# First layer: the first half's share of the second half's taps computed from PSUM, with a new order and new shares for the scan

## The chip, the cores and the metric

The kernel runs on one core of a Trainium2 chip. A core has five engines that work side by side, each through its own instructions in program order: TensorE (PE, matrix products and transposes, which land in PSUM), VectorE (DVE), ScalarE (ACT), GpSimd (POOL, which here works on SBUF alone) and SyncE (SP, which here issues the DMAs). In the profile, PEld is TensorE's loading of the stationary operand, which overlaps its products. The metric is the device time of one execution in microseconds (us).

## The reference, cut to what matters

Two layers run one after the other on `x`, float32 of shape (4, 512, 32, 32): four batches, 512 channels, 1024 positions. The change lies in the first one, a selective scan (Mamba) block with 1024 inner channels and 16 states.

```python
xz = xn @ W_in                                   # xn: normalized x, (B, L, 512)
xm, z = (xz[..., :d_inner], xz[..., d_inner:])
xc = conv_general_dilated(xm.transpose(0, 2, 1), conv_w[:, None, :], (1,), [(D_CONV - 1, 0)],
                          ..., feature_group_count=d_inner)   # 4 causal taps, channel by channel
xs = silu((xc + conv_b[None, :, None]).transpose(0, 2, 1))
proj = xs @ W_x
dt = softplus(proj[..., :dt_rank] @ W_dt + b_dt)
Bm = proj[..., dt_rank:dt_rank + D_STATE]
Cm = proj[..., dt_rank + D_STATE:]
A = -exp(A_log)
def step(h, inp):
    dt_t, B_t, C_t, x_t = inp
    dA = exp(dt_t[..., None] * A)
    h = dA * h + (dt_t * x_t)[..., None] * B_t[:, None, :]
    y = einsum('bds,bs->bd', h, C_t)
    return (h, y)
y = ys.transpose(1, 0, 2) + xs * D_param         # ys: the scan's y over all L positions
y = y * silu(z)
out = y @ W_out
```

Its output is added to `x`. The second layer (a position attention block with two 3x3 convolutions, which the kernel computes in a transformed form) follows.

## The kernel before, in words

**Tiling.** The 1024 inner channels are eight chunks `d` of 128 partitions. A pair of chunks is `e` (0 to 3), `j` tells the two of a pair apart, and the 1024 positions are two halves `h` of 512. The scan of a batch runs in eight stages, `n = 2e + h`, and each stage in 16 units, one for each state `s`; that makes 32 stages and 512 units. Products y are collected over the 16 states in two PSUM tiles by TensorE, with transposes that accumulate (line 985), and at a stage's end ScalarE copies them out (line 1008).

**A unit** needs exp(dt·A) (ScalarE, line 899), dt·x·B, the scan (DVE, two instructions at line 952), and the product with C. There are choices:
- dt·x·B is made by ScalarE in a transposed layout (four scalings, line 912) and turned by TensorE into PSUM (tile `u`, line 938), or by one POOL product over both chunks (line 927), for which B comes in by a broadcast DMA (tile `bbc`).
- The product with C, which a broadcast DMA brings (tile `cbc`), is one POOL instruction over both chunks (line 975) or two of DVE (line 968). For the first half, the scan's last column is kept in `carry_sb`, by POOL (line 974) or DVE (line 957).

How many of a stage's 16 units go by ScalarE is in the table `ACT_B` (a row for each batch, a column for each stage). How many of the others have their product with C on DVE is in `DVE_C`. The function `shares` spreads them over the states.

**The causal taps.** The first batch is started by halves: `conv1_half(d, h, prio)` projects a half of a chunk into PSUM (line 445, tile `pxm`), makes the tap without shift on ScalarE from PSUM into `u`, adds the three shifted taps on DVE (line 747) and applies SiLU (line 760). The first three positions of the second half need the last three columns of the first half. ScalarE keeps them in an SBUF tile `tails` (line 741), and when the second half comes, DVE adds their parts with three small instructions (line 752). The first halves of all chunks run first, and the second halves later, in between the first scan stage. The other batches are projected in one go by `conv1`, in three column ranges, with SiLU (line 719) for groups of chunks whose size is `PRM["xp"]`.

**Order.** All first-layer work is handed to a `Plan`. Each `step` names its engine, a cost in us, what it reads and writes, a priority (smaller is sooner), and the buffers that it holds. `Plan.issue` then runs a list schedule with these costs when the program is built, and emits the instructions in the order in which the schedule starts them. On the chip each engine keeps that order, whatever the true durations are. Priorities come from `PRM`: `kt`, `ke` and `ka` for how far the transposes, the exponentials and the additions to y lie ahead of their unit, `dl` for the deltas, `m0`, `c0`, `cg` and `p0` for the next batch's normalization and projections, `g0` and `gg` for the gates, `o0` and `og` for the output projection, `pc` for the 18 weight transforms of the second layer that are made in the first, `h0` and `hg` for the first batch's second halves, `l3` to `l6` and `fi` for the end. `TURN` and `URGENT` weigh a change of ScalarE's function table against the priority of what waits. The costs, such as `MM` (a matmul of 512 columns), `TR` (a transpose of 128), `ROWS` (two scalings), `EXP` and `SCAN`, stand in the code as numbers.

The second layer (lines from 1280 on) is written in plain order and runs after the first.

Of the kernel before, what the change touches and what calls it, by code (L numbers as in the profile page):

```python
# [15 lines left out]
P = 128  # L16
# [12 lines left out]


PRM = dict(
    xp=(2, 2, 1),
    d1=8.23,
    pg=(0.7, 0.35, 0.47, 0.46),
    kt=(1.13, 4.81, 2.25, 3),
    ke=(2.14, 5.78, 2.26, 3.85),
    ka=(-5.03, -1.69, -3.51, -2.93),
    dl=(11.85, 12.29, 12.5, 13.83),
    nl=(0.29, 0.79, 0.92),
    m0=(52.82, 51.61, 54.43),  # L40
    c0=(70.47, 60.11, 59.82),
    cg=(4.54, 5.65, 6.27),
    p0=(115.27, 106.44, 113.51),
    g0=(-0.87, -46.47, -49.33, -53.09),
    gg=(7.9, 8.99, 9.46, 7.52),
    o0=(15.94, 15.36, 9.69),
    og=(5.82, 6.15, 7.12),
    pc=(-120.93, -9.27, -95.57, -42.69, -26.91, -49.06, -36.73, 11.76, 16.43, 53.49, 94.05, 153.95, 217.99, 261.76, 328.41, 365.53, 443.31, 500.69),
    h0=-5.26,
    hg=2.44,  # L50
    p1=2.25,
    d2=-9.17,
    fl=0,
    fi=-3.13,
    l3=74.31,
    l5=104.57,
    l6=109.5,
)


ACT_B = (
# [4 lines left out]
)  # L66
DVE_C = (
# [4 lines left out]
)  # L72


# [22 lines left out]
class Plan:  # L97
# [5 lines left out]
    HOP = {"PE": 0.16, "DVE": 0.045, "ACT": 0.06, "POOL": 0.08, "SP": 0.05}  # L103
    BEGIN = {"PE": 5.0, "DVE": 1.5, "ACT": 9.0, "POOL": 7.0, "SP": 1.5}
    FREE, LOAD, SLACK, AHEAD = 0.06, 1.3, 0.11, 15.44
    TURN, URGENT = 2.11, 2.89

    def __init__(self, slots, in_order, exp_set):
        self.slots, self.steps, self.exp_set = dict(slots), [], exp_set
# [106 lines left out]
def mamba_then_pab_kernel(  # L216
# [105 lines left out]
    with ExitStack() as l0:  # L322
# [49 lines left out]


        carry_sb = wp.tile([P, 2, NS], F32, tag="carry", name="carry_sb")
        tails = wp.tile([P, NDC, 3], F32, tag="tails", name="tails")
        work = cpool.tile([P, NCC * (HH + 2) * (WW + 2)], F32, tag="image", name="work")
        proj_sb = wp.tile([P, L], F32, tag="proj", name="proj")
        nc.gpsimd.memset(proj_sb, 0.0)
# [19 lines left out]
            ("xt", "u", "h", "cbc", "bb", "dbx", "sc"), exp_set,  # L398
        )
        step = plan.step  # L400
        MM, TR = 0.858, 0.109
        ROWS, EXP, SCAN = 0.8, 0.613, 1.12

        def buf(ring, shape, name, free=False):
            if ring is None:
# [23 lines left out]

        xts, ready, xs, xh, dts = {}, {}, {}, {}, {}  # L430
        pieces = buf(None, None, "")
        tail = [buf(None, None, "") for d in range(NDC)]
        cells, at = {}, 0
        for ring, rows in (("tg", 9), ("tm", 6), ("tp", 6), ("tn", 6), ("to", 4), ("to", 4)):
            cells.setdefault(ring, []).append(work[:, at * QC : (at + rows) * QC])
# [16 lines left out]
        def norms(b, prio, lag=0.0):  # L452
# [167 lines left out]
            def scaled(c, h):  # L620
                hs = halves[h]
                step(
                    "DVE", 0.61,
                    lambda: nc.vector.scalar_tensor_tensor(
                        t()[:, c, hs], t()[:, c, hs], spl["nb"][:, c : c + 1], pvars[h](),
                        ALU.add, ALU.mult,
                    ),
                    [pvars[h], by_half[h]], [by_chunk[c][h]], prio, holds=[t],
                )
# [54 lines left out]
        def conv1(b, d, prio):  # L684

            w = load_win(b, d, prio)
            new_xs(b, d)
            u, xsh = xs[b, d], xh[b, d]
            cw = tap_weights(d)
            for at, end in ((0, 341), (341, 682), (682, L)):  # L690
                before = min(at, 3)
                n = end - at
                name = f"pxm_{b}_{d}_{at}"

                p = project(b, d, w, name, slice(at - before, end), prio, holds=[u])

                def tap(at=at, end=end, before=before, p=p):
                    nc.scalar.activation(
                        u()[:, at:end], p()[:, before : before + end - at], AF.Copy, scale=cw[0]
                    )  # L700

                step("ACT", 0.09 + n / 1000, tap, [p], xsh, prio, holds=[u])

                def taps(at=at, end=end, before=before, p=p):
                    for k in range(1, 4):
                        first = max(at, k)
                        nc.vector.scalar_tensor_tensor(  # L707
                            u()[:, first:end],
                            p()[:, first - k - at + before : end - k - at + before],
                            cw[k], u()[:, first:end], ALU.mult, ALU.add,  # L710
                        )

                step("DVE", 0.25 + n * 0.0037, taps, [p], xsh, prio, holds=[u])
        def silus(b, ds, prio):

            def several():
# [9 lines left out]
        def conv1_half(d, h, prio):  # L726

            if h == 0:
                new_xs(0, d)
            w, u, hs = load_win(0, d, prio), xs[0, d], halves[h]  # L730
            cw, me = tap_weights(d), [xh[0, d][h]]
            name = f"pxm_0_{d}_{h}"
            p = project(0, d, w, name, hs, prio, None if h else buf("u", [P, T], name, free=True), holds=[u])
            step(
                "ACT", 0.6,
                lambda: nc.scalar.activation(u()[:, hs], p(), AF.Copy, scale=cw[0]),
                [p], me, prio, holds=[u],
            )
            if h == 0:
                step(  # L740
                    "ACT", 0.2, lambda: nc.scalar.copy(tails[:, d], p()[:, T - 3 : T]),
                    [p], [tail[d]], prio,
                )

            def taps():
                for k in range(1, 4):
                    nc.vector.scalar_tensor_tensor(  # L747
                        u()[:, hs.start + k : hs.stop], p()[:, : T - k], cw[k],
                        u()[:, hs.start + k : hs.stop], ALU.mult, ALU.add,
                    )  # L750
                    if h:
                        nc.vector.scalar_tensor_tensor(
                            u()[:, T : T + k], tails[:, d, 3 - k :], cw[k],
                            u()[:, T : T + k], ALU.mult, ALU.add,
                        )

            step("DVE", 2.3 + 0.4 * h, taps, [p, *([tail[d]] if h else [])], me, prio, holds=[u])
            step(
                "ACT", 0.6,
                lambda: nc.scalar.activation(u()[:, hs], u()[:, hs], AF.Silu, bias=cb_sb[:, d : d + 1]),  # L760
                [], me, prio, "silu", holds=[u],
            )
# [118 lines left out]
        def unit(b, e, h, s, y):  # L881
# [50 lines left out]
            for j, u in enumerate(us):  # L932
                part = parts[j]
                if on_act:

                    def turn(j=j, u=u):
                        for k in range(NK):
                            nc.tensor.transpose(  # L938
                                u()[:, k * P : (k + 1) * P], sc()[:, k, j, :], ident
                            )  # L940

                    step(
                        "ACT", EXP, lambda j=j: decay(j, hc()[:, j]), [dt], [part], prio, "exp",
                        holds=[hc],
                    )
                    step("PE", 4 * TR, turn, [sc], [u], prio - PRM["kt"][b])
                else:
                    step("ACT", EXP, lambda j=j, u=u: decay(j, u()), [dt], [u], prio - PRM["ke"][b], "exp")

                def scan(j=j, u=u):  # L950
                    ht = u() if on_dve else hc()[:, j]
                    nc.vector.tensor_tensor_scan(  # L952
                        ht, *((hc()[:, j], u()) if on_act else (u(), hc()[:, j])),
                        carry_sb[:, j, s : s + 1] if h else 0.0, ALU.mult, ALU.add,
                    )
                    if h == 0 and on_dve:
                        nc.vector.tensor_copy(carry_sb[:, j, s : s + 1], ht[:, T - 1 : T])

                before, behind = ([carry[s][j]], []) if h else ([], [carry[s][j]] if on_dve else [])
                step(  # L960
                    "DVE", SCAN + (0.07 + 0.08 * (1 - h)) * on_dve, scan,
                    [part if on_act else hc, u, *before],
                    [u if on_dve else part, *behind], prio - 1, holds=[hc],
                )
                if on_dve:
                    step(
                        "DVE", 0.585,
                        lambda j=j, u=u: nc.vector.tensor_mul(hc()[:, j], u(), c_bc()[:, 0]),
                        [u, c_bc], [part], prio, holds=[hc],
                    )  # L970
            if not on_dve:
                def times_c():
# [2 lines left out]
                    nc.gpsimd.tensor_mul(hc(), hc(), c_bc().to_broadcast([P, 2, T]))  # L975

                step(
                    "POOL", 2.31 if h else 2.57, times_c,
                    [c_bc], [*parts, *([] if h else carry[s])], prio, holds=[hc],
                )  # L980
            for j in range(2):
# [237 lines left out]
        def transform(u, src, k, prio):  # L1219
# [16 lines left out]
            def scales():  # L1236
# [11 lines left out]
                [ends], [plus], prio, fill=True,  # L1248
            )
            step(  # L1250
                name, 1.76, lambda: eng.tensor_sub(minus(), plus(), mids()),
                [plus, mids], [minus], prio, fill=True,
            )
            step(
# [530 lines left out]
```

## Time and profile before

| | us |
|---|---|
| median of three runs | 2914.6 (2913.56 to 2916.33) |
| the profiled execution's own time | 2918.99 |
| its span, first to last instruction | 2917.2 |
| first layer, up to the first product of the second at 1892.8 | about 1893 |

The mean granted clock of TensorE is 0.983 of full speed. In the profile a group's row gives the line, engine, operation, tiles and shape, the count, the busy time and mean ns of one, and then the engine's idle time just before these instructions with what ended it. A row of waits has the engine and what it was to do, the work that released it, and the time in total, the times and the longest one. Tiles have the names of the program without numbers: `da` and `dbx` are a unit's SBUF tile (by ScalarE's way and by POOL's), `u` its PSUM tile.

### The profile page before, as it was taken

To read this page: it belongs to the slowest core of one execution; us is meant where nothing else is said; L and a number is where in the kernel's file an instruction comes from. 1 tells how busy PE (TensorE), PEld (TensorE's weight loads), DVE (VectorE), ACT (ScalarE), POOL (GpSimd) and SP (SyncE) were. 2 spreads that over 40 slices of the span, in tenths; PEclk is the share of its full clock that TensorE was granted. 3 is DMA by queue.
4 is the path that set the end of the run, shared out by engine and by line. 5 is a ranking of instruction groups with operands and counts; after the bars stand their busy time and mean duration, and the time that the engine had idled before them with its cause. 6 is when DMAs were issued, how large, how long until landed. Compare 5 with 4: busy or idle time off the path is not lost.

```text
span 2917.2 us, 36268 instructions
## 1 busy us (share of the span) xinstructions
PE 2728.5 (94%) x11744; PEld 1622.6 (56%) x11744; DVE 2315.5 (79%) x2762; ACT 1826.1 (63%) x3253; POOL 2001.9 (69%) x1217
## 2 busy tenths in 40 slices
PE   6798889999999999999999989799999999999998
PEld 3356566666666666666666766544444444444444
DVE  4579999998999989999899999867776755346254
ACT  4779899998989999989999999530300003030000
POOL 6889999889979999987999999733141341224222
PEclk9999899999999999999999999999999999999999
DMA  6665656568646578645576654667788896536487
GB/s 188 190 171 171 188 156 180 160 192 260 206 130 177 158 221 245 217 135 170 170 231 212 197 153 148 165 223 260 250 279 290 309 329 240 192 131 230 171 315 256
DMA packets 405829, 602.90 MB, mean 207 GB/s; under 512 B 47144, under 2 KB 246056, under 8 KB 381064
## 3 DMA queue, kind: packets, MB, share of 16 engines
q1 hardware_dynamic: 398024, 586.33, 63.3%
q10 hardware_dynamic: 7616, 14.26, 1.4%
q8 instruction: 94, 1.54, 0.2%
q14 instruction: 95, 0.78, 0.1%
HBM read 503.48 MB, written 96.99 MB: 206 GB/s over the span
## 4 chain that ended last, share of the span: by engine, by line
PE 33%; DVE 12%; ACT 4%; DMA 4%; POOL 3%; issue 2%; SPq 0%; DVEq 0%; POOLq 0%; ACTq 0%
PE m_o L1575 11%; PE m_b L1575 8%; PE pat L1627 4%; DVE da L952 3%; PE y L985 2%; PE po L445 2%; PE u L938 2%; DVE u L952 1%; POOL da L975 1%; ACT sc L912 1%; DVE xs L707 1%; PE psc L1427 1%; ACT da L899 1%; DMA u_o<-wo 1%; DMA uw_o<-u_o 1%
## 5 line engine op out<-in xcount | busy, mean ns | idle before, releaser
L975 POOL TENSOR_TENSOR da<-da,cbc 128x1024 f32<-128x1024 f32 x317 | 749.4, 2370 | 48.3 <-DVE da L952 26.6
L912 ACT ACTIVATE sc<-dtxt,bt_sb 128x256 f32<-128x256 f32 x1268 | 554.6, 497 | 35.4 <-PE u L938 34.4
L927 POOL TENSOR_TENSOR dbx<-dtx,bbc 128x1024 f32<-128x1024 f32 x195 | 461.1, 2375 | 31.7 <-PE y L985 21.6
L899 ACT ACTIVATE da<-dt,a_sb 128x512 f32<-128x512 f32 x634 | 436.5, 713 | 13.6 <-PE y L985 9.6
L938 PE MATMUL u<-ident,sc 128*128 128x128 f32 x2536 | 374.5, 280 | 50.7 <-DVE da L952 33.1
L938 PEld LDWEIGHTS u<-ident,sc 128*128 128x128 f32 x2536 | 294.8, 143 | 194.8 <-issue 51.3
L952 DVE TENSOR_TENSOR_SCAN da<-da,u 128x512 f32<-128x512 f32 x330 | 384.9, 1203 | 22.7 <-PE u L938 13.4
L952 DVE TENSOR_TENSOR_SCAN da<-da,carry_sb,u 128x512 f32<-128x512 f32 x304 | 372.9, 1261 | 16.5 <-PE u L938 9.5
L985 PE MATMUL y<-ident,da 128*128 128x128 f32 x2536 | 346.9, 277 | 26.1 <-POOL da L975 25.1
L1575 PE MATMUL m_o<-uw_o,v_o 128*128 128x512 f32 x768 | 335.4, 596 | 9.7 <-DMA uw_o<-u_o 9.7
L985 PEld LDWEIGHTS y<-ident,da 128*128 128x128 f32 x2536 | 294.3, 143 | 85.0 <-POOL da L975 42.1
L1575 PE MATMUL m_b<-uw_b,v_b 128*128 128x512 f32 x768 | 333.8, 593 | 5.7 <-DMA uw_b<-u_b 2.5
L899 ACT ACTIVATE u<-dt,a_sb 128x512 f32<-128x512 f32 x390 | 259.3, 682 | 18.8 <-DVE da L952 10.8
L445 PE MATMUL pxm<-xt,winc 128*128 128x345 f32 (+3 forms) x704 | 244.9, 490 | 13.0 <-DVE xs L707 3.8
L445 PE MATMUL pz<-xt,winc 128*128 128x512 f32 x512 | 243.1, 607 | 13.0 <-DVE xs L747 6.5
L1575 PEld LDWEIGHTS m_o<-uw_o,v_o 128*128 128x128 f32 x768 | 145.0, 191 | 191.6 <-issue 176.2
L1575 PEld LDWEIGHTS m_b<-uw_b,v_b 128*128 128x128 f32 x768 | 144.8, 190 | 191.2 <-issue 176.2
L1627 PE MATMUL pat<-y_b,st 128*128 128x512 f32 x512 | 223.3, 597 | 1.8 <-DVE rz L1636 1.8
L985 PE MATMUL y<-ident,dbx 128*128 128x128 f32 x1560 | 215.6, 277 | 10.0 <-POOL dbx L975 7.4
L985 PEld LDWEIGHTS y<-ident,dbx 128*128 128x128 f32 x1560 | 182.3, 143 | 39.4 <-issue 19.5
L1583 ACT ACTIVATE e_o<-m_o 128x512 f32<-128x512 f32 x24 | 14.3, 598 | 275.7 <-PE m_o L1575 261.3
L445 PE MATMUL po<-gt,wpr 128*128 128x512 f32 x384 | 182.5, 596 | 1.4 <-PE y L985 0.6
(225 smaller groups left out, 4241.6 us busy)
## 6 DMA issues: line engine op xcount, KB each, us to landing
cbc<-bcd SPq DMA_DIRECT2D x512, 256.0 KB, 3.7
uw_b<-u_b SPq DMA_DIRECT2D x96, 1024.0 KB, 4.8
uw_o<-u_o SPq DMA_DIRECT2D x96, 1024.0 KB, 4.7
bbc<-bcd SPq DMA_DIRECT2D x195, 256.0 KB, 4.3
u_b<-work SPq DMA_DIRECT2D x192, 128.0 KB, 3.1
winc<-in_w_in_dram SPq DMA_DIRECT2D x72, 256.0 KB, 3.9
szd<-sz SPq DMA_DIRECT2D x32, 512.0 KB, 4.5
szl<-szd SPq DMA_DIRECT2D x32, 512.0 KB, 4.9
```

The lines of the kernel that those rows point to most:

```text
L445: lambda k=k, lhs=lhs, rhs=rhs: nc.tensor.matmul(p()[:, at : at + cols], lhs(), rhs(), start=(k == 0), stop=(k == n - 1)),
L707: nc.vector.scalar_tensor_tensor(u()[:, first:end], p()[:, first - k - at + before : end - k - at + before], cw[k], u()[:, first:end], ALU ...
L899: nc.scalar.activation(t, dt()[:, j], AF.Exp, scale=a_sb[:, at : at + 1])
L912: nc.scalar.activation(sc()[:, k], dtxt()[:, k], AF.Copy, scale=bt[:, at, s : s + 1])
L927: lambda: nc.gpsimd.tensor_mul(hc(), dtx(), b_bc().to_broadcast([P, 2, T])),
L938: nc.tensor.transpose(u()[:, k * P : (k + 1) * P], sc()[:, k, j, :], ident)
L952: nc.vector.tensor_tensor_scan(ht, *((hc()[:, j], u()) if on_act else (u(), hc()[:, j])), carry_sb[:, j, s : s + 1] if h else 0.0, ALU.mul ...
L975: nc.gpsimd.tensor_mul(hc(), hc(), c_bc().to_broadcast([P, 2, T]))
L985: nc.tensor.matmul(y[j]()[:, k, :], hc()[:, j, k * P : (k + 1) * P], ident, start=(s == 0 and k == 0), stop=(s == NS - 1 and k == NK - 1), ...
L1427: nc.tensor.matmul(pt, top[:, m * P : (m + 1) * P], center[:, h * T : (h + 1) * T], start=True, stop=True,)
L1575: nc.tensor.matmul(m[q], v[:, q, k, c, :], w[:, c, :], start=(c == 0), stop=(c == NCC - 1 and not extra),)
L1627: nc.tensor.matmul(pt, st[m][:, 2 * P * j + h : 2 * P * (j + 1) : 2], xb[m // 2][:, m % 2, :], start=(m == 0), stop=(m == NMC - 1),)
```

## The change

- The `tails` tile and ScalarE's copies into it are gone. In the first half's tap step, DVE now reads the first half's last three columns from PSUM and writes their parts of the second half's first three positions straight into `u` (one multiplication, two multiply-adds). In the second half, ScalarE's unshifted tap leaves these three columns out, and DVE adds that tap there with one small instruction. The first half's step therefore also writes a part of the second half.
- `ACT_B` and `DVE_C` have new entries. Their sums by batch go from 73, 73, 78, 93 to 69, 76, 75, 94, and from 32, 31, 33, 25 to 32, 25, 25, 25.
- All of `PRM` has new numbers, `TURN` and `URGENT` too. `xp` is (1, 2, 1) instead of (2, 2, 1). A new entry `il` is read by no line shown.
- The costs of some steps are other numbers. They do not change what an instruction does, only the order in which the schedule puts it.

```diff
 PRM = dict(
-    xp=(2, 2, 1),
-    d1=8.23,
-    pg=(0.7, 0.35, 0.47, 0.46),
-    kt=(1.13, 4.81, 2.25, 3),
-    ke=(2.14, 5.78, 2.26, 3.85),
-    ka=(-5.03, -1.69, -3.51, -2.93),
-    dl=(11.85, 12.29, 12.5, 13.83),
+    xp=(1, 2, 1),
+    d1=10.1,
+    pg=(0.46, 0.4, 0.67, 0.61),
+    kt=(0.33, 3.93, 5.81, 6.9),
+    ke=(1.1, 4.93, 2.75, 4.55),
+    ka=(-4.81, -1.6, -3.24, 3.25),
+    dl=(9.79, 12.5, 12.12, 15.22),
...
-    fi=-3.13,
-    l3=74.31,
-    l5=104.57,
-    l6=109.5,
+    fi=-5.11,
+    l3=69.43,
+    l5=101.89,
+    l6=114.08,
+    il=0,
 )
 ACT_B = (
-    (12, 8, 10, 9, 10, 8, 8, 8),
-    (11, 8, 12, 9, 8, 9, 8, 8),
-    (11, 9, 13, 9, 10, 8, 9, 9),
-    (9, 11, 12, 12, 10, 13, 12, 14),
+    (12, 8, 10, 7, 9, 7, 8, 8),
+    (10, 12, 12, 8, 10, 8, 8, 8),
+    (12, 8, 13, 8, 9, 7, 10, 8),
+    (8, 13, 11, 13, 11, 13, 11, 14),
 )
 DVE_C = (
-    (3, 5, 6, 3, 1, 3, 5, 6),
-    (4, 7, 2, 3, 3, 5, 2, 5),
-    (5, 4, 3, 1, 5, 6, 3, 6),
-    (4, 3, 3, 4, 6, 1, 3, 1),
+    (2, 6, 6, 4, 1, 3, 5, 5),
+    (3, 4, 4, 4, 1, 4, 1, 4),
+    (4, 4, 3, 1, 1, 4, 1, 7),
+    (5, 2, 3, 1, 5, 3, 4, 2),
 )
...
-    TURN, URGENT = 2.11, 2.89
+    TURN, URGENT = 1.47, 1.72
...
-        MM, TR = 0.858, 0.109
-        ROWS, EXP, SCAN = 0.8, 0.613, 1.12
+        MM, TR = 0.875, 0.1135
+        ROWS, EXP, SCAN = 0.802, 0.615, 1.145
...
         def conv1_half(d, h, prio):
...
+            first = 3 * h
+
             step(
-                "ACT", 0.6,
-                lambda: nc.scalar.activation(u()[:, hs], p(), AF.Copy, scale=cw[0]),
+                "ACT", 0.575,
+                lambda: nc.scalar.activation(
+                    u()[:, hs.start + first : hs.stop], p()[:, first:], AF.Copy, scale=cw[0]
+                ),
                 [p], me, prio, holds=[u],
             )
-            if h == 0:
-                step(
-                    "ACT", 0.2, lambda: nc.scalar.copy(tails[:, d], p()[:, T - 3 : T]),
-                    [p], [tail[d]], prio,
-                )
 
             def taps():
+                if h:
+                    nc.vector.scalar_tensor_tensor(
+                        u()[:, T : T + 3], p()[:, :3], cw[0], u()[:, T : T + 3], ALU.mult, ALU.add
+                    )
                 for k in range(1, 4):
                     nc.vector.scalar_tensor_tensor(
                         u()[:, hs.start + k : hs.stop], p()[:, : T - k], cw[k],
                         u()[:, hs.start + k : hs.stop], ALU.mult, ALU.add,
                     )
-                    if h:
+                if h == 0:
+                    nc.vector.tensor_scalar_mul(u()[:, T : T + 3], p()[:, T - 3 :], cw[3])
+                    for k in (2, 1):
                         nc.vector.scalar_tensor_tensor(
-                            u()[:, T : T + k], tails[:, d, 3 - k :], cw[k],
-                            u()[:, T : T + k], ALU.mult, ALU.add,
+                            u()[:, T : T + k], p()[:, T - k :], cw[k], u()[:, T : T + k],
+                            ALU.mult, ALU.add,
                         )
 
-            step("DVE", 2.3 + 0.4 * h, taps, [p, *([tail[d]] if h else [])], me, prio, holds=[u])
-            step(
-                "ACT", 0.6,
+            both = xh[0, d] if h == 0 else me
+            step("DVE", 2.4 if h else 2.75, taps, [p], both, prio, holds=[u])
+            step(
+                "ACT", 0.63,
                 lambda: nc.scalar.activation(u()[:, hs], u()[:, hs], AF.Silu, bias=cb_sb[:, d : d + 1]),
                 [], me, prio, "silu", holds=[u],
             )
...
                 step(
-                    "DVE", SCAN + (0.07 + 0.08 * (1 - h)) * on_dve, scan,
+                    "DVE", SCAN + (0.04 + 0.14 * (1 - h)) * on_dve, scan,
...
                 step(
-                    "POOL", 2.31 if h else 2.57, times_c,
+                    "POOL", 2.326 if h else 2.59, times_c,
```

More of the change, by code (lines that the diff above doesn't have):

```diff
@@ L31 @@
 PRM = dict(
-    xp=(2, 2, 1),
-    d1=8.23,
-    pg=(0.7, 0.35, 0.47, 0.46),
-    kt=(1.13, 4.81, 2.25, 3),
-    ke=(2.14, 5.78, 2.26, 3.85),
-    ka=(-5.03, -1.69, -3.51, -2.93),
-    dl=(11.85, 12.29, 12.5, 13.83),
[L39 to L52, printed above, removed]
-    fl=0,
-    fi=-3.13,
-    l3=74.31,
-    l5=104.57,
-    l6=109.5,
+    xp=(1, 2, 1),
[5 more added lines that the diff above has]
+    dl=(9.79, 12.5, 12.12, 15.22),
+    nl=(0.17, 1.94, 1.25),
+    m0=(52.74, 50.42, 48.4),
+    c0=(68.39, 60.05, 64.33),
+    cg=(4.46, 6.19, 6.58),
+    p0=(117.51, 108.54, 112.88),
+    g0=(1.18, -46.47, -50.81, -55.84),
+    gg=(7.81, 8.86, 8.96, 7.61),
+    o0=(17.38, 16.29, 17.48),
+    og=(5.73, 4.85, 7.27),
+    pc=(-196.09, -39.49, -79.97, -11.49, -76.67, -112.89, -101.52, 31.36, 14.53, 57.53, 92.72, 155.74, 200.22, 264.5, 322.22, 362.01, 463.04, 499.85),
+    h0=-6.05,
+    hg=2.38,
+    p1=3.61,
+    d2=-7.19,
+    fl=0,
+    fi=-5.11,
[3 more added lines that the diff above has]
+    il=0,
 )
 ACT_B = (
[4 rows of a table removed]
[4 rows of a table added]
 )
 DVE_C = (
[4 rows of a table removed]
[4 rows of a table added]
 )
@@ L374, in mamba_then_pab_kernel @@
         carry_sb = wp.tile([P, 2, NS], F32, tag="carry", name="carry_sb")
-        tails = wp.tile([P, NDC, 3], F32, tag="tails", name="tails")
         work = cpool.tile([P, NCC * (HH + 2) * (WW + 2)], F32, tag="image", name="work")
@@ L431, in mamba_then_pab_kernel @@
         pieces = buf(None, None, "")
-        tail = [buf(None, None, "") for d in range(NDC)]
         cells, at = {}, 0
@@ L622, in scaled @@
                 step(
-                    "DVE", 0.61,
+                    "DVE", 0.658,
                     lambda: nc.vector.scalar_tensor_tensor(
@@ L711, in taps @@
                         )
-                step("DVE", 0.25 + n * 0.0037, taps, [p], xsh, prio, holds=[u])
+                step("DVE", 0.25 + n * 0.0042, taps, [p], xsh, prio, holds=[u])
         def silus(b, ds, prio):
@@ L966, in unit @@
                     step(
-                        "DVE", 0.585,
+                        "DVE", 0.59,
                         lambda j=j, u=u: nc.vector.tensor_mul(hc()[:, j], u(), c_bc()[:, 0]),
@@ L1250, in transform @@
             step(
-                name, 1.76, lambda: eng.tensor_sub(minus(), plus(), mids()),
+                name, 1.9, lambda: eng.tensor_sub(minus(), plus(), mids()),
                 [plus, mids], [minus], prio, fill=True,
```

## The prediction

> **What bounds the kernel now.** I read the page first, sections 1 and 2. TensorE (PE) is busy 94% of the span, but the slices show two regimes: in the first 26 slices PE, VectorE (DVE), ScalarE (ACT) and GpSimd (POOL) are all near nine tenths, and after that PE alone is. To find the borders I took the copies of the finished y tiles (line 1008) from the timeline, two to each of the 32 scan stages: the four batches end at about 601, 1047, 1504 and 1878 us, and the second layer starts at 1893. Then I asked for each engine's busy time in those stretches.
>
> ```profile
> PE 2728.5 (94%) x11744; PEld 1622.6 (56%) x11744; DVE 2315.5 (79%) x2762; ACT 1826.1 (63%) x3253; POOL 2001.9 (69%) x1217
> ...
> 0.00:100.00 100.00, 72.34 (x161) 29.95 (x162) 42.49 (x76) 47.10 (x81) 74.27 (x80) 0.97 0.67 186
> 100.00:601.00 501.00, 451.85 (x2352) 304.02 (x2350) 454.82 (x540) 453.88 (x787) 449.17 (x283) 0.96 0.58 172
> 601.00:1047.00 446.00, 419.74 (x2287) 286.37 (x2286) 415.57 (x486) 402.24 (x706) 404.95 (x245) 0.99 0.62 190
> 1047.00:1504.00 457.00, 438.11 (x2388) 301.14 (x2387) 429.20 (x512) 436.47 (x768) 408.96 (x250) 0.99 0.64 194
> 1504.00:1878.00 374.00, 339.38 (x2133) 250.65 (x2131) 358.49 (x388) 349.88 (x675) 359.81 (x221) 0.99 0.61 182
> 1893.00:2917.00 1024.00, 997.03 (x2404) 446.10 (x2404) 602.25 (x740) 135.43 (x238) 301.27 (x136) 0.99 0.71 249
> ```
>
> Columns: stretch, its length, then busy us of PE, PEld, DVE, ACT and POOL, the granted clock, DMA share and GB/s. The reader is to see that no engine alone bounds the first layer: in each batch the fullest one is 14 to 46 us short of the stretch, and those gaps are waits between engines whose order is fixed. So I read the waits of POOL and PE up to 1893 us next, then the rows of the operations that the change adds or removes:
>
> ```profile
> POOL carry_sb L974 <- DVE da L952: 43.8, 38, 4.1
> POOL da L975 <- DVE da L952: 26.6, 24, 4.1
> POOL dbx L927 <- PE y L985: 21.6, 15, 5.0
> ...
> PE u L938 <- DVE da L952: 33.1, 41, 2.9
> PE y L985 <- POOL da L975: 25.1, 27, 2.6
> ```
>
> ```profile
> L975 POOL TENSOR_TENSOR da<-da,cbc 128x1024 f32<-128x1024 f32 x317 | 749.4, 2370 | 48.3 <-DVE da L952 26.6
> ...
> L912 ACT ACTIVATE sc<-dtxt,bt_sb 128x256 f32<-128x256 f32 x1268 | 554.6, 497 | 35.4 <-PE u L938 34.4
> ...
> L968 DVE TENSOR_TENSOR dbx<-u,cbc 128x512 f32<-128x512 f32 x242 | 158.7, 673 | 2.2 <-DMA cbc<-bcd 2.2
> ...
> L741 ACT COPY tails<-pxm 128x3 f32<-128x3 f32 x8 | 1.2, 150 | 0.0
> ```
>
> The largest waits have a DVE scan (line 952) as their releaser: POOL stands 44 + 27 us for scans, PE 33 us for a scan to give back a PSUM tile. DVE is the engine that the others wait for.
>
> **The taps.** Per channel chunk d the change removes one ACT copy of three columns (150 ns; 8 of them, 1.2 us) and three DVE instructions of one to three columns in the second half. It adds three such to the first half and one to the second. In the timeline at 84 us the small ones take 0.12 to 0.3 us from start to next start, so the first half's DVE step grows by about 0.45 us per d and the second's shrinks by about 0.3; over all d, DVE +1 to +2 us. The first half lies at 48 to 79 us. There DVE sat idle 1.5 us before most tap steps while PE was busy 18.4 to 19.6 of each 20 us, so PE's projections cover the 0.45. Were that cover gone, it costs 8 x 0.45 = 3.6 us; a gain is bounded by the eight copies, 1.2 us. I take 0. A new wait: the first half's DVE step now also writes three columns of the second half, so the second half's ACT copy waits for it. It ended several us earlier (at 78.4 against 82.8 us in the trace), so ACT, with the deltas and exponentials queued behind, and the taps on DVE lose nothing. The PSUM tile of the first half comes free 0.45 us later, on PE's side, with four buffers in that ring.
>
> **The shares.** Every pair of chunks and state (512 units) takes dt·x·B through ACT and PE or as one POOL product, and the product with C on POOL or DVE. Summed by batch, the ACT table goes from 73, 73, 78, 93 to 69, 76, 75, 94, and the DVE table from 32, 31, 33, 25 to 32, 25, 25, 25. So POOL gets 4, -3, 3, -1 products with B more (+3) and 0, 6, 8, 0 products with C more (+14). One is 2.37 us (line 975): POOL +9, +7, +26, -2, together +40 us. DVE loses 14 x 2 products; on DVE the next instruction starts 0.60 us after one at 1010.5 us, so -7 and -10 us in batches 1 and 2, and nine fewer pairs of carry copies (158 ns each) take about 3 more. ACT: one unit's four scalings take 1.69 us in a row: -7, +5, -5, +2. PE: eight transposes in 1.04 us per unit: -4, +3, -3, +1. SP issues three more loads of 256 KB beside the 195 + 512 of that size.
>
> Here the trace and the Trainium skill weigh differently. By the rows, a product with C costs DVE 2 x 673 = 1346 ns and POOL 2370. "GPSIMD Engine Reference", section "Engine selection", says to put elementwise work on VectorE, GpSimd being about twice as slow with two inputs. By that rule the 14 moves are a loss of 14 x 1.02 = 14 us. By the waits they are none as long as POOL, idle 52, 41, 48 and 14 us in the four batches, has the room, and DVE, for which it waits, is done sooner. I take the trace's side, but keep the 14 for the range.
>
> **Tables on ACT.** Batch 1's SiLU goes chunk by chunk instead of in pairs: 8 steps for 4, up to 4 more loads of its table and 4 back. At 119 us and after, a load is 1.283 us (65 + 31 + 26 + 14 of them), so up to 10 us in batch 0's stretch. "ScalarE: Activation LUTs", section "What ACT_TABLE_LOAD costs", adds a drain of 1.38 us, which would make it 21. In the timeline the next ACTIVATE starts at 89.29, after a load of 1.28 begun at 88.00, which itself began right at the end of the instruction ahead. So no drain is seen, and I take half of the 10, since steps of one table can fall together. ACT in batch 0 is then about level: -7 - 1 + 5.
>
> **The order.** The trace of before cannot show what new priorities do; I bound it. A floor: if every batch's idle time stayed, its length would follow its fullest engine of DVE, ACT and POOL. That is 454.8 to 458 (POOL), 415.6 to 412 (POOL), 436.5 to 435 (POOL), 359.8 to 358.5 (DVE): +3, -4, -1, -1, sum -3 us. Above that stands the idle time itself, 46 + 30 + 21 + 14 = 111 us. The cost table under which the order was made had a scan at 1.12 us, while six scans at 1867.3 us take 7.11, about 1.18 each; over the 782 scans costed so (634 + 390 less 242 on units whose product is DVE's) that is near 50 us of DVE that the order did not reckon with. I read POOL's 70 us and PE's 33 as its trace. The new table has 1.145, a transpose 0.1135 for 0.109 and a 512-column matmul 0.875 for 0.858, nearer to the granted clock of 0.96 in batch 0. On top, DVE is relieved by 20 us in batches 1 and 2. I count a quarter of those 20, 5 us, as fewer waits, beyond the -3. A gain is capped by the idle: more than a third of 111, 37 us, I exclude, as an order that the engines keep only roughly never packs tightly. A loss is bounded by the rival below. Second layer: same instructions, 1024 us, 0. The stretch 1878 to 1893, where the image's normalization meets the last projections, moves by 1 us at most.
>
> **Sum.** Taps 0, load -3, waits -5: -8 us on the profiled execution's 2919.0 (span 2917.2 and 1.8 around it), hence 2911.0. The median of the runs, 2914.6, is 4.4 lower, and there the same step gives **2906.6**. A measurement of this kernel can tell about 0.2%, 5.8 us, from no change.
>
> **The rivals.**
> 1. The waits only change hands: DVE's 20 us are saved, but POOL at 435 of 457 us in batch 2 makes PE wait for its products as PE waited for scans (25 us already stand at "y <- POOL da"). Load -3, waits 0 to +6: 2909 to 2920, within 0.2%. For it: ACT, DVE and POOL together get 15 us more work, 5 each. Chance 0.2.
> 2. POOL becomes the bound, slower. In batch 2 it has 48 us idle and gets 26 more work, in batch 0 9 of 52. It decides from the point where its waits there cannot shrink below 48 - 26 = 22 us: 16 on PE's y, 11 and 9 on scans stood there, 36 in sum. If all 36 stay, 14 us go on the end, and in batches 0 and 1 some 4 to 8 of the 16 more: 2930 to 2937; half of it gives 2925. Against it: the scans that release 20 of the 36 come sooner. Chance 0.28, with a layout that meets other collisions on the chip.
> 3. The change does less than it says: impossible for the shares, which count instructions, but the tap edit alone is worth 0 either way, so a gain must be the layout's.
>
> **How the numbers follow.** My forecast: faster, 0.52, its own range 2888 to 2908. Same 0.2, slower 0.28. The range 2889 to 2930 leaves out about a tenth on each side: gains over 25 us and the full POOL case.
>
> **What the profile after would show.** Right: line 975 at 405 products and line 927 at 198; DVE about 2297 us busy, POOL about 2043; "POOL carry_sb, da <- DVE da" well under 70 us; the fourth batch's end at about 1870; no copy into tails, the first half's tap steps ending where PE still sets the pace. Wrong: PE's waits for POOL's da growing past 40 us, POOL over 96% full in batch 2 with that stretch longer than 457 us, more than 150 table loads, or a second layer other than 1024 us.

## The result and the profile after

The changed kernel takes 2893.8 us (median of three runs, 2890.95 to 2895.65) against 2914.6 before: 20.8 us less, a ratio of 0.9927 with a 95% interval of 0.9913 to 0.9941. Its profiled execution took 2893.83 us, with a span of 2892.0. That is 25.2 us less than the profiled execution of before, which was itself 4.4 us above its median.

The busy times of the whole span come first, then those by stretch, cut again at the copies of the finished y tiles (line 1013 now). The columns are those of before.

```profile
PE 2712.5 (94%) x11720; PEld 1614.8 (56%) x11720; DVE 2284.7 (79%) x2724; ACT 1837.3 (64%) x3249; POOL 2041.5 (71%) x1243
```

```profile
0.00:100.00 100.00, 70.33 (x161) 28.79 (x162) 46.20 (x97) 46.45 (x72) 72.33 (x78) 0.98 0.67 186
100.00:585.00 485.00, 438.86 (x2310) 295.11 (x2311) 436.22 (x519) 459.12 (x777) 457.71 (x289) 0.98 0.62 180
585.00:1022.00 437.00, 418.30 (x2315) 289.80 (x2313) 408.79 (x474) 410.31 (x724) 412.36 (x250) 0.99 0.62 193
1022.00:1487.00 465.00, 441.09 (x2364) 300.30 (x2362) 420.22 (x482) 434.29 (x758) 433.69 (x268) 0.98 0.62 188
1487.00:1856.00 369.00, 337.74 (x2144) 251.13 (x2144) 359.06 (x390) 350.33 (x681) 359.16 (x220) 0.99 0.63 188
1868.00:2892.00 1024.00, 996.62 (x2407) 445.85 (x2406) 603.65 (x747) 135.89 (x240) 305.84 (x142) 0.99 0.72 249
```

The stretches of the four batches are 485, 437, 465 and 369 us long instead of 501, 446, 457 and 374: three are shorter and that of batch 2 (batches count from 0) is longer. The gain begins very early. The y copies of the first two scan stages come at 185.4 and 236.4 us instead of 198.4 and 255.3, so 13 us are there by the end of the first stage and 19 by the end of the second. After that the lead, taken at the second copy of each stage, drifts between 13 and 35 us and is 22 us where the second layer begins (its first product is at 1871.0 instead of 1892.8). The last 3 us of the 25.2 lie in the second layer, whose instructions did not change: from its first product to the end it took 1021.0 us instead of 1024.4, and 1018.5 to 1024.4 over all profiled executions here, so they cannot be put down to the change.

These are the waits of POOL and PE in the first layer, and the rows of the operations that were moved:

```profile
POOL da L980 <- DVE da L957: 8.3, 11, 2.6
POOL carry_sb L979 <- DVE da L957: 7.9, 9, 2.5
...
PE y L990 <- POOL da L980: 28.5, 26, 3.2
PE u L943 <- DVE da L957: 19.0, 32, 2.1
```

```profile
L980 POOL TENSOR_TENSOR da<-da,cbc 128x1024 f32<-128x1024 f32 x314 | 742.3, 2370 | 33.0 <-DVE da L957 8.3
L917 ACT ACTIVATE sc<-dtxt,bt_sb 128x256 f32<-128x256 f32 x1256 | 550.6, 498 | 18.1 <-PE u L943 17.4
L932 POOL TENSOR_TENSOR dbx<-dtx,bbc 128x1024 f32<-128x1024 f32 x198 | 467.5, 2371 | 20.3 <-PE y L990 8.8
...
L980 POOL TENSOR_TENSOR dbx<-dbx,cbc 128x1024 f32<-128x1024 f32 x91 | 215.4, 2367 | 15.2 <-DVE dbx L957 6.9
```

POOL stood 70 us for scans on `da` tiles before and stands 16 now, while it has 40 us more to do (2041.5 against 2001.9).

**A row of before that matters.** The 24 small DVE instructions on `tails` had this in the list of groups of the kernel before:

```profile
L752 DVE SCALAR_TENSOR_TENSOR xs<-tails,cw_sb,xs 128x2 f32<-128x2 f32 x8 | 9.1, 1134 | 0.0
L752 DVE SCALAR_TENSOR_TENSOR xs<-tails,cw_sb,xs 128x1 f32<-128x1 f32 x8 | 6.2, 781 | 0.0
L752 DVE SCALAR_TENSOR_TENSOR xs<-tails,cw_sb,xs 128x3 f32<-128x3 f32 x8 | 5.7, 714 | 0.0
```

One to three columns take 0.7 to 1.1 us on average, 21.0 us in all. The timeline of before, with POOL beside DVE, shows why (start, duration, engine; other engines' rows are left out):

```profile
134.58 2.35 POOL L975 TENSOR_TENSOR da<-da,cbc 128x1024 f32<-128x1024 f32 x1
134.81 2.15 DVE L752 SCALAR_TENSOR_TENSOR xs<-tails,cw_sb,xs 128x1 f32<-128x1 f32 x1
...
136.90 2.34 POOL L927 TENSOR_TENSOR dbx<-dtx,bbc 128x1024 f32<-128x1024 f32 x1
...
137.53 1.73 DVE L752 SCALAR_TENSOR_TENSOR xs<-tails,cw_sb,xs 128x2 f32<-128x2 f32 x1
...
139.84 0.21 DVE L752 SCALAR_TENSOR_TENSOR xs<-tails,cw_sb,xs 128x3 f32<-128x3 f32 x1
```

The first ends at 136.96, POOL's product at 136.93; the second at 139.26, POOL's at 139.24; the third finds POOL idle and takes 0.21. The small instruction lasts until POOL's running one is over. This holds for all of the long ones: 16 of the 24 took more than 0.25 us, and each of the 16 ended within 0.03 us of the end of a POOL instruction. The inputs of these instructions, `tails` and `xs`, both lie in SBUF. In the changed kernel one of the two is a PSUM tile. The section "Who interferes with whom" of "SBUF — State Buffer" in the Trainium skill describes such a thing: VectorE's second SBUF read path is shared with GpSimd, an instruction with two SBUF inputs needs it, and whichever began first holds it for its whole length. That made it a theory to test.

### The profile page after: what moved, and what is told of

Same layout as the page of the kernel before. It is cut to its first block, busy times and chain, and to the rows that moved or that the text cites. A ratio compares the mean times of both kernels' runs of the same rounds, so it can differ in the third digit from the quotient of the medians.

```text
span 2892.0 us, 36189 instructions
## 1 busy us (share of the span) xinstructions
PE 2712.5 (94%) x11720; PEld 1614.8 (56%) x11720; DVE 2284.7 (79%) x2724; ACT 1837.3 (64%) x3249; POOL 2041.5 (71%) x1243
## 4 chain that ended last, share of the span: by engine, by line
PE 44%; ACT 21%; DVE 14%; POOL 9%; issue 7%; DMA 5%; SPq 0%; POOLq 0%; DVEq 0%; ACTq 0%
PE m_o L1580 11%; PE m_b L1580 8%; ACT sc L917 5%; PE y L990 4%; DVE da L957 4%; PE pat L1632 4%; ACT da L904 4%; POOL da L980 4%; PE u L943 4%; PE po L444 3%; ACT u L904 3%; PE pxm L444 2%; PE pz L444 2%; ACT L251 2%; POOL dbx L932 1%
## 5 line engine op out<-in xcount | busy, mean ns | idle before, releaser
L932 POOL TENSOR_TENSOR dbx<-dtx,bbc 128x1024 f32<-128x1024 f32 x198 | 467.5, 2371 | 20.3 <-PE y L990 8.8
L943 PE MATMUL u<-ident,sc 128*128 128x128 f32 x2512 | 362.3, 278 | 32.8 <-DVE da L957 19.0
L990 PE MATMUL y<-ident,da 128*128 128x128 f32 x2512 | 338.4, 276 | 29.3 <-POOL da L980 28.5
L980 POOL TENSOR_TENSOR dbx<-dbx,cbc 128x1024 f32<-128x1024 f32 x91 | 215.4, 2367 | 15.2 <-DVE dbx L957 6.9
```

The source lines that it names most:

```text
L932: lambda: nc.gpsimd.tensor_mul(hc(), dtx(), b_bc().to_broadcast([P, 2, T])),
L943: nc.tensor.transpose(u()[:, k * P : (k + 1) * P], sc()[:, k, j, :], ident)
L990: nc.tensor.matmul(y[j]()[:, k, :], hc()[:, j, k * P : (k + 1) * P], ident, start=(s == 0 and k == 0), stop=(s == NS - 1 and k == NK - 1), ...
```

## The experiments

The prediction had put the tap edit at 0 and the gain in the layout (shares, priorities, costs). The first four kernels take one part each out of the changed kernel. The ratios of all experiments are against the kernel before, run on the same chip. Where the order is kept, the planner's steps and costs are untouched and only what some steps emit differs; where a kernel is laid out anew, the planner makes a new order from the edited numbers.

### The old taps in the new order

The plan's steps, costs and thus the order are those of the changed kernel. Only what two steps emit is old.

```diff
-  u()[:, hs.start + first : hs.stop], p()[:, first:], AF.Copy, scale=cw[0]
+  u()[:, hs], p(), AF.Copy, scale=cw[0]       # and, for h == 0, in the same step:
+  nc.scalar.copy(tails[:, d], p()[:, T - 3 : T])
...
-  the small instructions that read p()
+  nc.vector.scalar_tensor_tensor(u()[:, T : T + k], tails[:, d, 3 - k :], cw[k], ...)   # h == 1
```

> The changed kernel with its order kept step by step, but with the old tap instructions: eight copies into tails back on ScalarE, three small DVE instructions per chunk in the second half. Theory (the gain is the layout, the taps are covered by PE's projections): 2894 us, within 3 us of the changed kernel's 2893.8, ratio 0.992 to 0.994. Rival (the taps bring part of the 13 us that the first scan stage gained): 2899 to 2907, ratio 0.995 or more.

Measured: 2907.4 us, ratio 0.9967 (0.9955 to 0.9980). From 0.9927 to 0.9967 is 0.40%, some 12 us: more than half of the gain is the tap edit's, and the rest, 0.33% or near 10 us, is the layout's. The y copy of the first scan stage comes at 196.8 us, 11 us later than in the changed kernel, and the distance stays at 11 us to the fourth batch's end (1867.2 against 1855.8).

### Old shares, old costs, old priorities

```diff
 e2: ACT_B and DVE_C as before
 e3: MM, TR, ROWS, EXP, SCAN and the other changed costs as before (not those of the first batch's taps)
 e4: PRM, TURN and URGENT as before
```

> The changed kernel with the old tables ACT_B and DVE_C, laid out anew with its priorities and costs. Theory A (the relief of DVE by 20 us and the truer costs each bring a part): about half of the 21 us is lost, 2900 to 2908. Theory B (priorities and shares are one fitted set; shares that do not belong to the priorities fit nowhere): all of it and more is lost, 2914 to 2935. Theory C (shares bring nothing, only costs and priorities): 2892 to 2898.

> The changed kernel with the old cost numbers for the steps outside the first batch's taps (scan 1.12, matmul 0.858, transpose 0.109 and so on), laid out anew with its priorities and shares. Theory A (the order is better because it reckons with the scan's true time): 2903 to 2915, and POOL's waits for scans come back to 40 us or more from 16. Theory B (one fitted set): 2910 to 2930, whatever the waits. Theory C (the costs hardly matter): 2892 to 2898.

> The changed kernel with the old priorities (PRM, TURN, URGENT), new shares and costs. Theory A: costs and shares alone keep half of the gain: 2900 to 2908. Theory B (one fitted set): the old priorities belong to the old shares and costs, 2914 to 2935, slower than before.

Measured: 2953.9 us (1.0123, 1.0103 to 1.0143), 2923.4 (1.0028, 1.0019 to 1.0036) and 2940.2 (1.0076, 1.0058 to 1.0094). Each is slower than the kernel before, although each keeps the tap edit and two of the three other parts. All three go the way of theory B, though e2 and e4 lost more than its ranges allowed (up to 2935). In e3 POOL's waits for scans on `da` come to 34 us, short of the 40 that theory A expected.

### The new taps in the old order

```diff
-  lambda: nc.scalar.activation(u()[:, hs], p(), AF.Copy, scale=cw[0]),
+  lambda: nc.scalar.activation(u()[:, hs.start + 3 * h : hs.stop], p()[:, 3 * h :], AF.Copy, scale=cw[0]),
...
-  "ACT", 0.2, lambda: nc.scalar.copy(tails[:, d], p()[:, T - 3 : T]),
+  "ACT", 0.2, lambda: None,
...
   taps() as in the change; costs and dependencies of the steps as before
```

> The kernel before, its order kept step by step, with the new tap instructions alone. In the run with the old taps in the new order, single small instructions on the tails tile (two inputs in SBUF) took up to 2.2 us and ended when POOL's running instruction ended. Theory (these stalls are what the tap edit takes away, in either order): 10 to 14 us faster than before, 2902 to 2906, ratio 0.995 to 0.9965, all of it by the end of the second scan stage. Rival (the 12 us belonged to the new order, which was laid out for the shorter second tap step): within 4 us of before, ratio 0.9985 or more.

Measured: 2905.2 us against 2915.8, ratio 0.9958 (0.9941 to 0.9975): 10.6 us faster. The y copies of the first two stages come at 186.2 and 243.7 us, 12 us earlier than before, as expected. So the tap edit is worth some 10 to 12 us in either order.

### Small instructions with two SBUF inputs, and their twins with one

Both kernels are the changed one with its order. After each of the second half's shifted taps DVE gets one more small instruction, on a spare tile whose values nobody uses.

```diff
+  if h:
+      nc.vector.scalar_tensor_tensor(
+          spare[:, 4 : 4 + k], spare[:, :k], cw[k], spare[:, 4 : 4 + k], ALU.mult, ALU.add   # e6
+          spare[:, 4 : 4 + k], p()[:, :k],   cw[k], spare[:, 4 : 4 + k], ALU.mult, ALU.add   # e7
+      )
```

> The changed kernel, order kept, with three extra small DVE instructions per chunk in the second half (one, two, three columns, results unused), both inputs in SBUF. Theory (an instruction with two SBUF inputs waits for POOL's running one): most of the 12 us that the old taps cost comes back, 2902 to 2910, and these 24 instructions take 0.8 us each on average. Rival (it is only the number of small instructions): 24 x 0.2 = 5 us of DVE, 2894 to 2899, the same as the twin with one PSUM input.

> The twin: the same three extra small DVE instructions per chunk, of the same sizes, but with one input in PSUM and one in SBUF. Theory (contention with POOL): they take 0.2 us each, 2893 to 2898. Rival (number alone): as slow as the twin with two SBUF inputs.

Measured: 2903.1 us, ratio 0.9954 (0.9937 to 0.9971), with two SBUF inputs, and 2894.7, ratio 0.9927 (0.9912 to 0.9941), with one. Count, sizes and places are the same. These are the groups of the first and then of the second kernel:

```profile
L756 DVE SCALAR_TENSOR_TENSOR spare<-spare,cw_sb 128x2 f32<-128x2 f32 x8 | 7.9, 987 | 0.0
L756 DVE SCALAR_TENSOR_TENSOR spare<-spare,cw_sb 128x3 f32<-128x3 f32 x8 | 6.7, 843 | 0.0
L756 DVE SCALAR_TENSOR_TENSOR spare<-spare,cw_sb 128x1 f32<-128x1 f32 x8 | 6.6, 823 | 0.0
```

```profile
L756 DVE SCALAR_TENSOR_TENSOR spare<-pxm,cw_sb,spare 128x2 f32<-128x2 f32 x8 | 1.7, 211 | 0.0
L756 DVE SCALAR_TENSOR_TENSOR spare<-pxm,cw_sb,spare 128x3 f32<-128x3 f32 x8 | 1.7, 211 | 0.0
L756 DVE SCALAR_TENSOR_TENSOR spare<-pxm,cw_sb,spare 128x1 f32<-128x1 f32 x8 | 1.7, 209 | 0.0
```

With one PSUM input none of the 24 takes more than 0.22 us; with two SBUF inputs they take 21.2 us in sum, up to 1.98. In the timeline of the second kernel one runs right inside a POOL product and is not held:

```profile
131.42 2.37 POOL L938 TENSOR_TENSOR dbx<-dtx,bbc 128x1024 f32<-128x1024 f32 x1
...
132.14 0.21 DVE L756 SCALAR_TENSOR_TENSOR spare<-pxm,cw_sb,spare 128x1 f32<-128x1 f32 x1
```

So where the second input lies makes the difference, and the 24 small instructions by themselves cost nothing that could be measured (0.9927 with them and without). The stalls alone are worth 8.4 us between the twins. That is most of the 10.6 to 12 us of the tap edit; no run splits the rest, in which the eight ACT copies and the places of the instructions differ too.

### The new shares alone, and nudged costs

```diff
 e8:  kernel before, new ACT_B and DVE_C
 e9:  changed kernel, SCAN 1.145 -> 1.147
 e10: changed kernel, TR 0.1135 -> 0.1137
 e11: kernel before, SCAN 1.12 -> 1.122
```

> The kernel before with the new tables ACT_B and DVE_C alone, laid out anew by its own costs and priorities. Theory A (relief of DVE by 20 us is a gain in itself): 2905 to 2912. Theory B (shares and priorities are one fitted set): 2920 to 2945, slower than before, although DVE has 20 us less to do.

> The changed kernel with one cost number moved by 0.2%: a scan at 1.147 instead of 1.145 us, laid out anew; instructions, shares and priorities are the same. Theory B (the 10 us of the layout are those of one picked order among many, to which the numbers were fitted): most of them is lost, 2903 to 2925, as with larger edits. Theory A (truer costs and relief of DVE give an order that is better in general): 2890 to 2900.

> The changed kernel with the cost of a transpose at 0.1137 instead of 0.1135 us, laid out anew. Theory B: 2903 to 2925. Theory A: 2890 to 2900.

> The kernel before with a scan at 1.122 instead of 1.12 us, laid out anew. Theory B (before is a picked order as well): slower than before by 5 to 30 us, 2920 to 2945. Theory A: within 6 us of before, 2909 to 2921.

Measured: e8 2940.4 us (1.0081, 1.0066 to 1.0096), e9 2923.6 (1.0020, 1.0009 to 1.0031), e10 2905.2 (0.9959, 0.9945 to 0.9974), e11 2939.6 (1.0074, 1.0059 to 1.0089). A cost moved by 0.2% changes the order on PE, DVE, ACT and POOL and costs 0.3 to 0.9% by the ratios, 9 to 27 us, with the same computation and the same shares. All four lie in the ranges of theory B: both kernels behave like picked orders, each faster than every re-laid neighbour of it that was run (five of the changed kernel, two of the kernel before).

## Why the prediction was right, and where its sum was not

**Direction and range: right.** Faster was the likeliest case, and 2893.8 lies in its own range of 2888 to 2908. The forecast of 8 us was too small by 13. More than half of the gain came from a term put at 0. The layout alone, 0.9967 of 2914.6 or some 2905 us, would have met the forecast of 2906.6 closely, but in part by luck, since the account behind it does not hold (below).

**The term that was mis-sized: the taps, taken at 0, measured at -10.6 us in the old order and -12 in the new one.** The step that failed is the prediction's reading of the small instructions "at 84 us", 0.12 to 0.3 us each, and the bound on a gain "by the eight copies, 1.2 us". At 84 us POOL ran short products of the weight transforms (0.73 us each). From 119 us on it ran products of 2.37 us, and there the same instructions took up to 2.15. The row of all 24 (781, 1134 and 714 ns on average) was not used. What the edit saves is 24 stalled instructions, 21.0 us, against eight with a PSUM input in the second half at 0.21 us, 1.7 us. Of these 19 us of DVE time, more than half reaches the end, all of it in the first scan stages, where the second halves' taps stand in DVE's queue between scans. "DVE +1 to +2 us" had the wrong sign for the same reason: with the old order kept (e5), DVE is busy 13 us less. Over the whole change its busy time fell by 30.8 us, where the sum had 18. The part on the first halves was right in the main: their step is longer by three instructions of 0.21 to 0.22 us, 0.75 us from start to start instead of 0.45, and in the old order the first two second halves begin only 1.8 and 0.3 us later (84.6 and 98.6 us instead of 82.8 and 98.4).

**Load and waits, -8 us, measured -10 for the layout as a whole.** With the taps old in the new order the ratio is 0.9967, 9.6 us. The sizes of the shares were right: 405 and 198 POOL products, POOL busy 2041.5 us where some 2043 were expected. The account by batches was not: -16 and -9 us in the first two, where the floor had +3 and -4, and batch 2 longer by 8. In batch 2 POOL is 93% full (433.7 of 465 us). A stretch over 457 us with POOL over 96% full was named as a sign of the slower case; the length came, the 96% did not, and the other batches outweigh it.

**A reading behind the waits was wrong.** The six scans at 1867 us, 1.18 us each, are second halves, which read `carry_sb`, and their figure was taken for all 782 scans of that cost. The rows of before tell the two kinds apart:

```profile
L952 DVE TENSOR_TENSOR_SCAN da<-da,u 128x512 f32<-128x512 f32 x330 | 384.9, 1203 | 22.7 <-PE u L938 13.4 <-ACT da L899 9.2
L952 DVE TENSOR_TENSOR_SCAN da<-da,carry_sb,u 128x512 f32<-128x512 f32 x304 | 372.9, 1261 | 16.5 <-PE u L938 9.5 <-ACT da L899 6.9
```

From one start to the next it is 1.12 us for first halves on average, just the old cost, and 1.18 for second halves. There are 386 of these (304 in the second row and 82 on `dbx`), so the old order missed some 23 us of DVE and not "near 50". The new 1.145 is nearer to the mean of both, but too long for the one kind and too short for the other.

**The cause inside the layout is not settled.** The waits that were to shrink did shrink. If all of POOL's waits in which a scan releases a tile `da` or `dbx` are summed (up to 1868 us), they are 79 us before, 26 after, 42 with the old taps in the new order and 72 with the new taps in the old order. So the order took away 37 to 46 us of them, and the 40 us of products that POOL got fill that time. But short waits are not the gain: they are 46 us in e9, 37 in e10 and 43 in e3, well under the 79 of before, and with the tap edit in them too, e9 and e3 are slower than before and e10 gains no more than the tap edit alone. And the runs with parts exchanged show that neither the new shares (e8) nor truer costs (e3 without them is slower, and so is e9 with one made slightly larger) are a gain in themselves. Only the fitted set is, and its two nudged neighbours took 2905 and 2924 us. As far as these runs show, the 10 us are the difference between two picked orders; what in the order makes them stays open. Whether the new costs give better orders on average was not tried; one nudge of the old set (2940) and two of the new one are too few to say.

**Rivals.** That the waits only change hands holds in part: PE's wait for POOL's `da` grew from 25 to 28.5 us, while its wait for scans fell from 33 to 19. POOL as the bound did not come to pass: in batch 0 it got 9 us more work in a stretch that is 16 us shorter. The third, that the tap edit is worth nothing and a gain must be the layout's, is refuted by e1 and e5.

**Tables on ACT.** "More than 150 table loads" was to be a sign of the slower case. There are 157 instead of 141, 20.5 us more of ACT at 1.283 us each, and the kernel is faster. Twelve of the 16 lie in batch 0's stretch, where ACT is now the fullest engine, at 459 of 485 us. The term of +5 us of ACT's time was too small by 10 there, and the stretch is 16 us shorter in spite of it; what the loads by themselves cost was not tried. The drain that would have doubled it is not seen here either: in the profile after, a load begins 0.02 us after the end of the instruction ahead and the next instruction starts 0.01 us after the load (medians of the 157).

## What to carry to other kernels

Look up the mean of every instruction that an edit removes over all of its places, not in one stretch: a row whose mean is several times what its size explains points to a stall, for which the row itself shows no wait. When GpSimd is busy, try giving VectorE's short instructions one input from PSUM where there is a choice; here the small SBUF copies of a PSUM tile, made "to be read later", cost most of 10 us in the instructions that read them. And when an order is written out by a planner, compare an edit with the order held fixed, since a cost number nudged by 0.2% made the time 0.3 to 0.9% longer here.

## What the runs showed of the hardware that was not expected

- A DVE instruction of one to three columns with both inputs in SBUF lasted up to 2.15 us beside a POOL product, and each of the 16 longest ended within 0.03 us of a POOL instruction. With one input in PSUM the same one took 0.21 us in 24 of 24 cases.
- A POOL product beside it is not slowed: 2.35 and 2.34 us in the two cases shown, against a mean of 2.37.
